# Moving small condition networks, phi matrices and a weight's transposes to other places in a planned schedule, and letting two copies choose their engine

## The chip, the cores and the metric

The kernel runs on one NeuronCore of a Trainium2 chip, as a single program in fp32. The metric is the device time of one execution in microseconds (us), lower is better. Five queues matter: TensorE (PE, matmuls and transposes into PSUM), VectorE (DVE), ScalarE (ACT, activations), GpSimd (POOL, which here also issues the indirect DMAs) and SyncE (SP, which issues the other DMAs). Each queue runs its instructions in the order in which they stand in the program; they meet through semaphores.

## The reference

Two layers, 32 samples of 256 tokens with 256 features, 8192 tokens in all. Layer 0 is a modulated linear, attention and a two-choice mixture of 8 experts with at most 2048 tokens each. Layer 1, which is where the change lies, is cut here to what it touches:

```python
# L1 attention: q and k pass through a phi matrix per head (attn_weights) and a global norm
# L1_cond2: six views of x, concatenated, then a two-layer network
def _mlp_ln(s, W1, b1, W2, b2, g, b):
    h = jax.nn.silu(s @ W1 + b1) @ W2 + b2
    return _ln(h, g, b)
m = x + _mlp_ln(memory_state, mem_W1, ...)[:, None, :]      # cond_512, 32 x 128
n = x + _mlp_ln(noise_state, noi_W1, ...)[:, None, :]       # cond_64,  32 x 64
r = x + _mlp_ln(resource_state, res_W1, ...)[:, None, :]    # fside,    32 x 32
w = jax.nn.softmax(aw)
cat = jnp.concatenate([w[0]*h, w[1]*t, w[2]*m, w[3]*n, w[4]*r, w[5]*s], axis=-1)
z = _mlp_ln(cat, int_W1, int_b1, int_W2, int_b2, int_g, int_be)
# L1 feed-forward: a linear, ten butterfly stages, gelu, ten butterfly stages, a linear
h = butterfly(z @ W_exp + b_exp, up_weights, 1024)
h = butterfly(gelu(h + up_bias), down_weights, 1024)
y = h @ W_con + b_con + down_bias
```

The three condition networks (`mem`, `noi`, `res`) work on 32 rows in all: one row per sample. Each is two small matmuls, a silu, a layer norm and a transpose.

## The kernel before, in words

**The stages.** The first stage (to about 1700 us in the trace) is layer 0's attention and routing. Then one planned section holds everything else: the expert blocks (to about 2676 us), the first pass over layer 1 (`answer`, one part per sample, to about 2847 us), a short chain that needs all samples (`norms`, global norms of q and k), and the second pass (`answer_out`, one part per sample, to the end).

**What sets the order.** All work of this section is written as Python generators, called parts. A part yields steps: an engine with an estimated length, then issues that step's instructions; a wait of an estimated length with no engine (`yield None, 2.5`); a buffer of a ring (`get`), given back with `back`; `("join", part)`, which holds the part until another part has ended. `side_by_side` plays all parts against its estimates as a list scheduler, and the order in which it lets steps go is the order of the instructions in each queue. Two engines in one yield, such as `yield (ACT, 0.7), (DVE, 0.75)`, leave the choice to it: it takes the one that ends first by its own estimates. Nothing is reordered on the chip: a step that was planned early and is ready late holds up all that stands behind it on its engine.

**Rings.** The planned section has 20 buffers `sh` of 128 x 512, 11 `big` of 128 x 2048 and 8 PSUM banks `mm`. A load of a weight into an `sh` buffer waits in SP's queue until that buffer's former user is through.

**Experts.** `expert_block` handles 512 slots: four gathers on POOL (L1529), transposes (L1539), eight hidden tiles `bh` (L1573, relu on ACT or DVE at L1560/L1562), two pairs of output tiles `by` (L1588), the bias (DVE, L1594), the gate (L1603), and four scatter-adds into the residual in memory by POOL (L1496). The scatter-adds go one at a time: each waits for the landing of the one before. All `answer` parts wait for all blocks and all scatter-adds, then load their tokens `x2` by SP (L1729) and transpose them on PE (helper `transpose2`, L246).

**What the change touches.** `butterflies` works up the two feed-forward weights during the experts; at its end it transposes the second one on PE (L1690, four groups of four) and copies it from PSUM to `w_con` on DVE (L1694). `small_tables` waits for `butterflies` and then, in one sequence: loads bias rows; computes the phi matrices `waq` and `abq` from three small weights (L1859 and L1869 on PE, copies L1864 and L1871 on DVE); loads `iw1`, the first weight of the six-view network, scales it by a softmax (ACT, L1902 to L1914; POOL, L1917, L1918); runs the three condition networks one after the other (loads L1927 to L1932; PE L1937, L1946, L1963; silu on ACT L1941; DVE L1952 to L1954, L1959, L1967; the power -1/2 on POOL, L210 and L216); and adds them up into `bvec` (PE L1979, DVE L1986). Every network holds five `sh` buffers. `norms` waits for all of `answer`, `squares`, `small_tables` and `butterflies`.

`answer_out` does, per sample: two projections (L266), softmax-like features, a layer norm, side views `t` and `s` on POOL (L2047, L2049) and `h` on DVE, transposes of `x`, `t`, `s`, `h` (L246), the copy of `h` from PSUM (DVE, L2134), 16 matmuls over the six-view weight (L2147), silu (ACT, L2156), a projection, a layer norm (`un`), its transposes, the scale and bias of `zT` from PSUM (DVE, L2175), 16 matmuls `dh` with gelu (L2198, L2188), 16 matmuls `do` (L2212) and the output. Up to four samples are in flight.

Of the kernel before, what the change touches and what calls it, by code (L numbers as in the profile page):

```python
# [14 lines left out]
F = mybir.dt.float32  # L15
# [7 lines left out]
P = 128  # L23
S = 256
D = 256
# [144 lines left out]
def network(ctx: ExitStack, tc: tile.TileContext, a: dict, out: bass.AP):  # L170
# [113 lines left out]
    def back(r):  # L284
        return "back", rings[r][2]
# [1354 lines left out]
    def butterflies(after):  # L1640

        for p in after:
            yield "join", p
        xb = yield from get("big", "bfb", [1, FF])
        yield SP, 0.1
        nc.sync.dma_start(w_eff, a["wexp"].rearrange("(c p) f -> p c f", p=P))
        yield SP, 0.1
        nc.sync.dma_start(xb, a["bexp"])
        for st in range(NST):
            w = yield from get("big", "bfw", [P, FF // 2, 2, 2])  # L1650
            yield SP, 0.1
            nc.sync.dma_start(
                w.rearrange("p k i j -> p (k i j)"), a["upw"][st : st + 1, :].to_broadcast([P, 2 * FF])
            )
            yield DMA, 5.3
            yield None, 2.0
            for x in (w_eff[:, 0, :], w_eff[:, 1, :], xb):
                yield from butterfly_stage(x, w, 1 << st, False)
            yield back("big")

        ps = yield from get("mm", "mm", [P, 8])
        yield PE, 0.6
        for f in range(8):
            nc.tensor.matmul(
                ps[:, f : f + 1], xb[0:1, f * P : (f + 1) * P], ones[0:1, 0:1], start=True, stop=True
            )
        yield DVE, 0.2
        nc.vector.tensor_add(b_eff, ps, cols[:, C_UPB : C_UPB + 8])
        yield back("mm")
        yield back("big")  # L1670
        xw = yield from get("big", "bfx", [P, 2, FF])
        yield SP, 0.1
        nc.sync.dma_start(xw, a["wconT"].rearrange("(c p) f -> p c f", p=P))
        for st in reversed(range(NST)):
            w = yield from get("big", "bfw", [P, FF // 2, 2, 2])
            yield SP, 0.1
            nc.sync.dma_start(
                w.rearrange("p k i j -> p (k i j)"), a["dnw"][st : st + 1, :].to_broadcast([P, 2 * FF])
            )
            yield DMA, 5.3  # L1680
            yield None, 2.0
            for c in range(2):
                yield from butterfly_stage(xw[:, c, :], w, 1 << st, True)
            yield back("big")
        for f in range(0, 8, 2):
            ps = yield from get("mm", "mm", TS)
            yield PE, 0.55
            for g in range(2):
                for c in range(2):
                    nc.tensor.transpose(  # L1690
                        ps[:, g, c * P : (c + 1) * P], xw[:, c, (f + g) * P : (f + g + 1) * P], ident
                    )
            yield DVE, 0.7
            nc.vector.tensor_copy(w_con[:, f : f + 2, :], ps)  # L1694
            yield back("mm")
        yield back("big")

# [128 lines left out]
        yield back("big")  # L1826
        yield back("big")

    def small_tables():

        yield "join", weights_part
        yield "join", matrices
        yield SP, 0.1
        nc.sync.dma_start(rowsD, a["rows_d"][:, :N_ROWS_D].to_broadcast([P, N_ROWS_D]))
        bb = yield from get("sh", "bb")
        yield SP, 0.1
        nc.sync.dma_start(
            bb.rearrange("p t d -> p (t d)"), a["rows_d"][:, N_ROWS_D : N_ROWS_D + 2 * D].to_broadcast([P, 2 * D])
        )
        yield None, 2.5  # L1840
        yield DVE2, 0.5
        nc.vector.tensor_add(bcon, bb[:, 0, :], bb[:, 1, :])
        yield back("sh")
        yield POOL, 0.1
        nc.gpsimd.memset(qacc, 0.0)

        blk = yield from get("sh", "blk", [P, 2, P])
        yield SP, 0.1
        nc.sync.dma_start(blk, a["ablk"].rearrange("(k p) m -> p k m", p=P))
        for n in ("aq", "ak"):  # L1850
            nat = yield from get("sh", "nat")
            yield SP, 0.1
            nc.sync.dma_start(nat, a[n].rearrange("(k p) i -> p k i", p=P))
            yield None, 2.5
            for i in range(2):
                ps = yield from get("mm", "mm", TS)
                yield PE, 0.9
# [15 lines left out]
            yield back("sh")  # L1873
        yield back("sh")


        awr = wD.tile([P, 6], F, name="awr")
        wsm = wD.tile([P, 6], F, name="wsm")
# [2 lines left out]
        awo = ROWS_S["aw"][0]  # L1881
        yield SP, 0.1
        nc.sync.dma_start(awr, a["rows_s"][:, awo : awo + 6].to_broadcast([P, 6]))
        condin = {}
        for n, src, k in (("mem", "condT", P), ("noi", "noiT", 64), ("res", "resT", 32)):
            if n == "mem":
                condin[n] = condT
            else:
                condin[n] = wD.tile([k, B], F, name="ci_" + n)
                yield SP, 0.1  # L1890
                nc.sync.dma_start(condin[n], a[src])
        iw1 = []
        for i in range(2):
            t = yield from get("big", "iw1", [P, 6, D])
# [20 lines left out]
        for k in range(2):  # L1915
            yield POOL, 1.3
            nc.gpsimd.tensor_add(wcat[:, 6 + k, :], iw1[4 + k], iw1[6 + k])  # L1917
            nc.gpsimd.tensor_add(wcat[:, 6 + k, :], wcat[:, 6 + k, :], iw1[8 + k])  # L1918
        vT = {}
        for n in ("mem", "noi", "res"):  # L1920
            ci = condin[n]
            k = ci.shape[0]
            m1 = yield from get("sh", "m1", [k, D])
            m2 = yield from get("sh", "m2")
            rb = yield from get("sh", "rb", [B, D])
            yield SP, 0.1
            nc.sync.dma_start(m1, a[n + "W1"])  # L1927
            yield SP, 0.1
            nc.sync.dma_start(m2, a[n + "W2"].rearrange("(k p) n -> p k n", p=P))
            o, w_ = ROWS_S[n + "b2"]  # L1930
            yield SP, 0.1
            nc.sync.dma_start(rb, a["rows_s"][:, o : o + w_].to_broadcast([B, w_]))  # L1932
            yield None, 2.5
            ps = yield from get("mm", "mm", TS)
            yield PE, 0.4
            for m in range(2):
                nc.tensor.matmul(ps[:, m, :B], m1[:, m * P : (m + 1) * P], ci, start=True, stop=True)  # L1937
            hT = yield from get("sh", "mhT", [P, 2, B])
            yield ACT, 1.8
            for m in range(2):  # L1940
                nc.scalar.activation(hT[:, m, :], ps[:, m, :B], AF.Silu, bias=col(n + "b1", m))  # L1941
            yield back("mm")
            ps = yield from get("mm", "mm", TS)
            yield PE, 0.9
            for c in range(2):
                nc.tensor.matmul(ps[:B, 0, :], hT[:, c, :], m2[:, c, :], start=(c == 0), stop=(c == 1))  # L1946
            u = yield from get("sh", "mu", [B, D])
            st = sm.tile([B, 6], F, name="mst")
            mv = sm.tile([B, 2], F, name="mmv")
            rstd = sm.tile([B, 1], F, name="mrs")  # L1950
            yield DVE, 1.1
            nc.vector.tensor_add(u, ps[:B, 0, :], rb)  # L1952
            nc.vector.bn_stats(st, u)
            nc.vector.bn_aggr(mv, st)  # L1954
            yield back("mm")
            yield POOL, 0.8
            rsqrt(rstd, mv[:, 1:2], 1, LN_EPS)
            yield DVE, 0.4
            nc.vector.tensor_scalar(u, u, mv[:, 0:1], rstd, ALU.subtract, ALU.mult)  # L1959
            ps = yield from get("mm", "mm", TS)  # L1960
            yield PE, 0.3
            for c in range(2):
                nc.tensor.transpose(ps[:, c, :B], u[:, c * P : (c + 1) * P], ident[:B, :B])  # L1963
            vT[n] = wD.tile([P, 2, B], F, name="vT_" + n)
            yield DVE, 0.3
            for c in range(2):
                nc.vector.tensor_scalar(  # L1967
                    vT[n][:, c, :], ps[:, c, :B], col(n + "g", c), col(n + "be", c), ALU.mult, ALU.add
                )
            yield back("mm")  # L1970
            for _ in range(5):
                yield back("sh")
        ps = yield from get("mm", "mm", TS)
        yield PE, 1.6
        for m in range(2):
# [84 lines left out]
    def answer_out(b, begin, before):  # L2060
# [69 lines left out]
        yield PE, 0.55  # L2130
        transpose2(ps, h2)
        cT["h"] = yield from get("sh", "cT_h", TS)
        yield DVE, 0.7
        nc.vector.tensor_copy(cT["h"], ps)  # L2134
        yield back("mm")
        yield back("sh")
        for p in (px, pt, ps_):
# [32 lines left out]
        transpose2(ps, un)  # L2170
        yield back("sh")
        zT = yield from get("sh", "zT", TS)
        yield DVE, 0.9
        for c in range(2):
            nc.vector.tensor_scalar(  # L2175
                zT[:, c, :], ps[:, c, :], col("intg", c), col("intbe", c), ALU.mult, ALU.add
            )
        yield back("mm")


        yield "rank", B
        gT = yield from get("big", "gT", [P, 8, S])

        def gelu(ps, f0):
# [51 lines left out]
    table_part = Part(small_tables())  # L2236
    first_parts = [Part(answer(b)) for b in range(B)]
    square_part = Part(squares() if NG > 0 else iter(()))
    norm_part = Part(norms([*first_parts, square_part, table_part, matrices]))
    with tc.manual_schedule():  # L2240
        side_by_side(
            [routed, weights_part, *loads[:2], matrices, *blocks, *loads[2:], table_part, *first_parts, square_part, norm_part]
# [126 lines left out]
```

## Time and profile before

| | us |
|---|---|
| median of 3 runs | 3804.84 (3804.16 to 3808.98) |
| the profiled execution, its own time | 3813.55 |
| its span in the profile | 3811.8 |
| PE busy in the span | 3516.6 (92%) |
| DVE / ACT / POOL busy | 2519.2 (66%) / 1796.2 (47%) / 1810.6 (48%) |

The granted TensorE clock has a mean of 0.97 over the span. Read the page as follows: part 1 gives the busy time of each engine; part 2 cuts the span into 40 slices and shows where an engine is not full; part 4 follows the chain that ended last. PE is the fullest engine and carries 41% of that chain. In part 2 its row has the digit 9 nearly everywhere after the first slices and 8 or 7 in two places: around 1700 us, where routing is, and in the slices from 2600 us and from 2800 us, on both sides of the first pass over layer 1.

A matmul or a transpose in fp32 is recorded as two matmul records, except transposes, of which there is one per instruction; the time that a group of them takes from PE is best read from the distance between the starts of neighbouring rows, since their ends are modelled.

### The profile page before, as it was taken

Reading aid. Unit: us, or ns where it says so; the run is one execution under the profiler, and the core shown is the slowest. Engines: PE = TensorE matmul, PEld = TensorE weight load, DVE = VectorE, ACT = ScalarE, POOL = GpSimd, SP = SyncE. Lnnn points to the kernel's source line nnn. Section 1 sums busy time; section 2 is a strip of 40 time slices with the busy share of each in tenths; the row PEclk is TensorE's granted clock in tenths of the full one; section 3 lists DMA queues with packets and bytes.
Section 4 is the critical chain, followed back from the end, with each engine's and each line's share of the span. In section 5 each row is a group of like instructions: output and inputs, shape, how many; then the busy total and the mean of one; then the engine's idle time right before and its main releaser. Section 6 shows DMA issues by size and latency. Waiting matters only on the chain.

```text
span 3811.8 us, 55412 instructions
## 1 busy us (share of the span) xinstructions
PE 3516.6 (92%) x22001; PEld 2582.0 (68%) x22001; DVE 2519.2 (66%) x4296; ACT 1796.2 (47%) x2714; POOL 1810.6 (48%) x1291
## 2 busy tenths in 40 slices
PE   3899999999999999987999999999898999999999
PEld 2566666666666666654666666666787888888888
DVE  7999998899898899746665551000336656565654
ACT  2677777777777777752222222222332333333333
POOL 3436543544544444415555565553125556565553
PEclk7999999999999999987999999999999999999999
DMA  1001000000100000004333333322341233222321
GB/s 63 18 29 33 30 30 22 26 31 27 30 30 30 30 30 25 25 18 156 88 85 102 82 97 76 65 43 38 117 163 56 100 96 109 91 92 91 122 92 42
DMA packets 136494, 241.43 MB, mean 63 GB/s; under 512 B 19265, under 2 KB 80897, under 8 KB 133666
## 3 DMA queue, kind: packets, MB, share of 16 engines
q0 software_dynamic: 48128, 100.77, 10.8%
q1 hardware_dynamic: 87954, 136.51, 10.7%
q8 instruction: 176, 2.88, 0.3%
q14 instruction: 92, 0.75, 0.1%
q10 hardware_dynamic: 144, 0.52, 0.0%
HBM read 187.25 MB, written 50.48 MB: 62 GB/s over the span
## 4 chain that ended last, share of the span: by engine, by line
PE 41%; DVE 5%; issue 4%; POOL 3%; DMA 1%; ACT 0%; SPq 0%; POOLq 0%; DVEq 0%; ACTq 0%
PE by L1588 11%; PE bh L1573 11%; PE do L2212 4%; PE mm L2147 4%; PE dh L2198 3%; PE mm L266 3%; PE mm L246 1%; PE mm L258 1%; PE gram L1762 1%; PE mm L1539 1%; DVE st L315 1%; POOL ga L2035 1%; DVE v L2110 1%; DVE hh L2049 0%; POOL gc L2035 0%
## 5 line engine op out<-in xcount | busy, mean ns | idle before, releaser
L975 ACT ACTIVATE pt<-sc 128x2048 f32<-128x2048 f32 x256 | 481.1, 1879 | 160.1 <-PE sc L966 157.3
L216 POOL TENSOR_TENSOR n<-n,negh 128x32 f32<-128x32 f32 x64 | 377.1, 5893 | 200.9 <-DVE n L827 151.6
L216 POOL TENSOR_TENSOR rstd<-rstd,negh 128x2 f32<-128x2 f32 x160 | 146.0, 914 | 673.3 <-DVE rstd L317 668.9
L1562 ACT ACTIVATE hid<-bh,cols 128x512 f32<-128x512 f32 x256 | 175.2, 688 | 599.2 <-PE bh L1573 586.1
L1588 PE MATMUL by<-w,hid 128*128 128x256 f32 x2048 | 454.5, 380 | 2.5 <-DVE ysb L1594 2.5
L1573 PE MATMUL bh<-ehT,w 128*128 128x512 f32 x1024 | 451.4, 594 | 1.3 <-DVE ysb L1594 1.3
L1588 PEld LDWEIGHTS by<-w,hid 128*128 128x128 f32 x2048 | 387.6, 191 | 67.2 <-issue 14.4
L948 PE MATMUL av<-pt,vaug 128*32 128x256 f32 x4096 | 280.7, 392 | 81.0 <-ACT pt L975 73.9
L1594 DVE TENSOR_TENSOR ysb<-by,b 128x512 f32<-128x512 f32 x64 | 44.0, 688 | 457.0 <-PE by L1588 379.8
L1573 PEld LDWEIGHTS bh<-ehT,w 128*128 128x128 f32 x1024 | 194.7, 191 | 221.3 <-issue 215.2
L1496 POOL DMA_INDIRECT rrows<-ysb,row x128 | 220.5, 1723 | 256.9 <-DMA rrows<-ysb,row 148.5
L786 DVE TENSOR_TENSOR hprod<-hprod 128x1024 f32<-128x1024 f32 (+2 forms) x384 | 319.4, 832 | 6.5
L966 PE MATMUL sc<-qT,kT 32*128 32x256 f32 x4096 | 299.2, 407 | 6.1 <-ACT pt L975 6.0
L778 DVE TENSOR_TENSOR hprod<-hex,kk 128x2048 f32<-128x2048 f32 x128 | 296.3, 2315 | 0.0
L966 PEld LDWEIGHTS sc<-qT,kT 32*128 32x128 f32 x4096 | 188.2, 187 | 104.0 <-issue 88.2
L948 PEld LDWEIGHTS av<-pt,vaug 128*32 128x32 f32 x4096 | 108.2, 110 | 208.7 <-ACT pt L975 118.8
L2198 PE MATMUL dh<-zT,w_eff 128*128 128x256 f32 x1024 | 237.2, 381 | 6.7 <-DVE zT L2175 6.7
L2212 PE MATMUL do<-w_con,gT 128*128 128x256 f32 x1024 | 232.6, 381 | 0.0
L1529 POOL DMA_INDIRECT xg<-h2buf,tok x128 | 152.3, 1190 | 162.9 <-issue 55.8
L2198 PEld LDWEIGHTS dh<-zT,w_eff 128*128 128x128 f32 x1024 | 190.2, 191 | 31.3 <-DVE zT L2175 7.9
L2212 PEld LDWEIGHTS do<-w_con,gT 128*128 128x128 f32 x1024 | 194.0, 192 | 25.6
L735 DVE TENSOR_REDUCE hex<-hprod 128x64 f32<-128x1024 f32 (+1 forms) x192 | 176.1, 948 | 2.4
(615 smaller groups left out, 7128.7 us busy)
## 6 DMA issues: line engine op xcount, KB each, us to landing
w<-in_w SPq DMA_DIRECT2D x16, 1024.0 KB
x<-rrows SPq DMA_DIRECT2D x64, 256.0 KB
bfw<-in_upw SPq DMA_DIRECT2D x10, 1024.0 KB
bfw<-in_dnw SPq DMA_DIRECT2D x10, 1024.0 KB
xT<-in_xT SPq DMA_DIRECT2D x32, 256.0 KB
x<-in_x SPq DMA_DIRECT2D x32, 256.0 KB
ugbb<-gtab SPq DMA_DIRECT2D x32, 256.0 KB
h2buf<-xh SPq DMA_DIRECT2D x32, 256.0 KB
```

The lines of the kernel that those rows point to most:

```text
L216: nc.gpsimd.tensor_tensor(o, o, negh[:p].to_broadcast([p, n]), ALU.pow)
L735: nc.vector.tensor_reduce(e[:, t, j0 : j0 + n, :] if exact else e[:, t, 8:, j0 : j0 + n].rearrange("p h j -> p j h"), pr[:, t].rearrange(" ...
L778: nc.vector.tensor_tensor(pr.rearrange("p j (h d) -> p j h d", d=DH), weights(t, j0, 8)[:, 0].unsqueeze(3).to_broadcast([P, 8, H, DH]), wi ...
L786: nc.vector.tensor_tensor(pr[:, :n], pr[:, :n], pr[:, n : 2 * n], ALU.add)
L948: nc.tensor.matmul(av[32 * i : 32 * i + 32, c % 2, :], va[:, kc, 4 * c + i, :], pt[:, i, kc, :], start=(kc == 0), stop=(kc == 1),)
L966: nc.tensor.matmul(sc[:, i, kc, :], kT[r, m, kc * P : (kc + 1) * P], qT[r, e, m, :], start=True, stop=nm is None,)
L975: nc.scalar.activation(pt, sc, AF.Exp, scale=1.0 / math.sqrt(DH))
L1496: nc.gpsimd.indirect_dma_start(rrows[:, :], bass.IndirectOffsetOnAxis(ap=row[:, j0 + t : j0 + t + 1], axis=0), y[:, t, :], None, compute_o ...
L1573: nc.tensor.matmul(ps, w["w1"][:, c, f * P : (f + 1) * P], hT[c], start=(c == 0), stop=(c == 1))
L1588: nc.tensor.matmul(ps[:, t, :], hid[f // 4][:, f % 4, (t0 + t) * P : (t0 + t + 1) * P], w["w2"][:, f, :], start=(f == 0), stop=(f == 7),)
L2198: nc.tensor.matmul(ps[:, g, :], w_eff[:, c, f * P : (f + 1) * P], zT[:, c, :], start=(c == 0), stop=(c == 1))
L2212: nc.tensor.matmul(ps[:, t, :], gT[:, f, t * P : (t + 1) * P], w_con[:, f, :], start=(f == 0), stop=(f == 7))
```

## The change

- The phi part of `small_tables` becomes a part of its own, `phi_weights`. Its loads are issued first, and its PE work joins the last expert block (`blocks[-1]`).
- The three condition networks become parts of their own, `condition_network`, which run beside each other. Their loads are issued early; their PE work, too, joins the last expert block. Their instructions are the same.
- `small_tables` no longer waits for `butterflies`, but for the fourth block from the end (`blocks[-4]`); it starts the networks and the phi part, then goes on with `iw1` and its scaling, and joins them before `bvec`.
- In `butterflies`, the transposes of the second linear wait for the first `NG + 2` parts `answer` (30 of 32), and their copies move from DVE to ACT. `norms` no longer waits for `butterflies`; each `answer_out` does, ahead of its gelu.
- In `answer_out` two copies out of PSUM, `cT_h` and `zT`, may go to DVE or ACT.

```diff
@@ butterflies
+        for p in first_parts[: NG + 2]:
+            yield "join", p
         for f in range(0, 8, 2):
...
-            yield DVE, 0.7
-            nc.vector.tensor_copy(w_con[:, f : f + 2, :], ps)
+            yield ACT, 0.6
+            nc.scalar.copy(w_con[:, f : f + 2, :], ps)
@@ small_tables, its phi part
-        yield "join", weights_part
-        yield "join", matrices
...
+    def phi_weights():
         blk = yield from get("sh", "blk", [P, 2, P])
...
+        yield None, 2.5
+        yield "join", blocks[-1]
+        for n, nat in zip(("aq", "ak"), nats):
@@ small_tables, its networks
+    def condition_network(n, src, k, vT):
...
+        m1 = yield from get("sh", "m1", [k, D])
+        m2 = yield from get("sh", "m2")
+        rb = yield from get("sh", "rb", [B, D])
...
+        yield None, 2.5
+        yield "join", blocks[-1]
+        ps = yield from get("mm", "mm", TS)
+        yield PE, 0.4
...
+    def small_tables():
+        yield "join", weights_part
+        yield "join", blocks[-4]
...
+        vT = {}
+        nets = [Part(condition_network(*n, vT)) for n in (("mem", "condT", P), ("noi", "noiT", 64), ("res", "resT", 32))]
+        for p in nets:
+            yield p
+        phis = Part(phi_weights())
+        yield phis
...
-        for n in ("mem", "noi", "res"):
...
+        for p in (*nets, phis):
+            yield "join", p
@@ answer_out
-        yield DVE, 0.7
-        nc.vector.tensor_copy(cT["h"], ps)
+        engine = yield (DVE, 0.7), (ACT, 0.6)
+        if engine == ACT:
+            nc.scalar.copy(cT["h"], ps)
+        else:
+            nc.vector.tensor_copy(cT["h"], ps)
...
-        yield DVE, 0.9
+        engine = yield (DVE, 0.9), (ACT, 1.0)
         for c in range(2):
...
+            if engine == ACT:
+                nc.scalar.activation(
+                    zT[:, c, :], ps[:, c, :], AF.Identity, bias=col("intbe", c), scale=col("intg", c)
+                )
...
         yield "rank", B
+        yield "join", matrices
         gT = yield from get("big", "gT", [P, 8, S])
@@ network
-    norm_part = Part(norms([*first_parts, square_part, table_part, matrices]))
+    norm_part = Part(norms([*first_parts, square_part, table_part]))
```

## Prediction, on record before the run

> **What bounds the kernel now.** I read the page first: PE is busy 92% of the span and carries 41% of the chain that ended last, so a stage gets shorter only where PE gets less to do or waits less. Then I cut the span into stretches of 100 us and looked for those where PE is not full. The columns are the stretch, its length, the busy time of PE, PEld, DVE, ACT and POOL, the granted clock, the DMA share and GB/s.
>
> ```profile
> 2500.00:2600.00 100.00, 100.00 (x362) 66.36 (x361) 9.30 (x21) 23.32 (x35) 51.18 (x43) 1.00 0.28 48
> 2600.00:2700.00 100.00, 86.41 (x345) 62.71 (x344) 12.35 (x33) 28.36 (x54) 29.19 (x25) 0.91 0.23 45
> 2700.00:2800.00 100.00, 98.56 (x599) 86.86 (x597) 37.85 (x88) 29.36 (x69) 13.89 (x43) 1.00 0.45 151
> ```
>
> The experts (2500) and the first pass over layer 1 (2700) are full. Between them lies a hole. PE's own order of time shows it (start, duration, line, work, count; in brackets the idle time before and who ended it):
>
> ```profile
> 2660.03 0.61 PE L1859 MATMUL mm<-blk,nat 128*128 128x128 f32 x4
> 2660.48 7.07 PE L1588 MATMUL by<-w,hid 128*128 128x256 f32 x32
> 2667.39 0.50 PE L1869 MATMUL mm<-cols,blk 128*128 128x1 f32 x4
> 2667.75 7.15 PE L1588 MATMUL by<-w,hid 128*128 128x256 f32 x32
> 2674.74 1.05 PE L1859 MATMUL mm<-blk,nat 128*128 128x128 f32 x8
> 2675.63 0.51 PE L1869 MATMUL mm<-cols,blk 128*128 128x1 f32 x4
> 2688.94 1.97 PE L246 MATMUL mm<-ident,x 128*128 128x128 f32 x8 [12.81 <-DMA x<-rrows]
> ...
> 2700.71 0.53 PE L1937 MATMUL mm<-condT,m 128*128 128x32 f32 x4
> 2701.07 0.63 PE L252 MATMUL mm<-ident,yT 128*128 128x128 f32 x4
> ...
> 2703.36 1.05 PE L1946 MATMUL mm<-m,mhT 128*32 128x256 f32 x4
> 2704.34 1.58 PE L1762 MATMUL gram<-y 128*128 128x257 f32 x8
> ```
>
> The last expert tile ends at 2674.74 and the first token tile of layer 1 is there at 2688.94. What sets this is not PE: the last four scatter-adds start at 2668.94, 2673.42, 2677.85 and 2682.35 on POOL, each after the landing of the one before, SP issues the loads at 2686.32, and they land 2.6 us later. So PE work put into this hole is free, and the same work in the full stages around it is not. The reader is to see that two pieces of phi (L1859, L1869) stand in full stretches before the hole, and all of the networks (L1937 and on) in the full stretch after it.
>
> The last stage, 2884 to the end, has smaller holes. PE's waits there (who waited for whom: us in total, times, longest):
>
> ```profile
> PE dh L2198 <- DVE zT L2175: 6.7, 3, 2.2
> PE mm L246 <- POOL s L2049: 5.7, 9, 1.9
> PE mm L246 <- DVE h L2049: 5.6, 4, 1.7
> PE mm L246 <- POOL t L2049: 3.3, 3, 1.8
> PE mm L246 <- DVE un L238: 3.2, 4, 1.1
> PE mm L246 <- POOL x L2112: 2.8, 5, 0.7
> ```
>
> Together 27.3 us of 928. A zT stall in its place: PE ends the transposes of `un` near 3319.1, but DVE has two `hh` steps queued first (the second takes 1.64), so zT starts at 3320.90.
>
> **Phi matrices.** From the starts of neighbouring rows: 0.45 (2660.03 to 2660.48), 0.36 (2667.39 to 2667.75) and a first group at 2632.04, 0.44. These 1.25 us leave the full stage. The rest of phi, 1.4 us after 2674.74, lies in the hole already. Gain 1.25. Its DVE copies (0.42 and 0.15 each) move into the hole, where DVE is nearly idle.
>
> **Networks.** One network costs PE 0.36 (L1937), 0.98 (L1946, 2703.36 to 2704.34) and 0.23 (L1963, 2708.61 to 2708.84) = 1.57; three cost 4.71, in a stage where PE is 98.6% busy. In the built order of the changed kernel all three stand behind the last `by`, except for one last L1963 and one L1859, which stand behind five token tiles: 0.23 + 0.36 stay. Gain 4.71 - 0.59 = 4.1.
>
> Does the chain hold up the token tiles, which stand behind it on PE? Count from the end of the last `by`, T. The built order puts the three powers on POOL behind the last scatter-add, whose issue ends at T + 9.2 (2683.90). A power is 0.18 + 0.58, two take 1.7; DVE's normalization is 0.40, PE's transposes follow. The second transposes, the last thing ahead of the tiles, are reached near T + 11.8; the tiles land at T + 14.2 or a little later. Slack about 2.5 us: cost 0. The third network follows behind five tiles and is then ready (its power near T + 13.5).
>
> Everything else that a network issues: three or four loads on SP (0.3 to 0.6 each). They now stand ahead of `iw1` and wait for `sh` buffers: in the built order the last such wait is for the pair of scatter-adds that landed at 2592.78 in this trace, the very event that let SP go on to `iw1` before. So `iw1` lands about as before (DMA falls idle again near 2604.5), plus some 1.2 us for 0.4 MB more. Silu (0.28 each, six) and its table load (1.28) leave the busy pass for the hole.
>
> **`iw1`.** Its 12 scalings (4.89) and six copies (1.92 in the rows of ACT) and four POOL adds (0.72 to 1.31) ran in the hole; the built order puts them ahead of the relus of the block before the last. ACT has 7.5 us free there (it ends at 2605.41 and needs its next relu at 2612.88), POOL 8.0 us before its next scatter-add (2612.52). What falls there, 6.0 us (two scalings come earlier) and 3.5, fits: cost 0. Without that cover, the relus would wait for ACT by up to 6 us.
>
> **Transposes of the second linear.** 16 at 0.11 us = 1.76 us (2296.56 to 2296.99 for four). They leave a full stage, but in the built order they stand ahead of the last squares of the first pass, which is full as well. Net 0 (from -1.8 if they meet a pause to +2.4 if the four ACT copies, 0.59 each by the row of `y`, delay the last squares; nearer to 0, since ACT waits 18 us for PE there).
>
> **A rule about the clock.** In this trace the granted clock drops within the hole and stays low into the pass:
>
> ```profile
> 2676.00:2678.00 2.00, 0.13 (x2) 0.05 (x1) 1.56 (x9) 0.30 (x1) 0.15 (x1) 1.00 0.28 41
> 2680.00:2682.00 2.00, 0.00 (x0) 0.00 (x0) 0.00 (x0) 2.00 (x6) 0.00 (x0) 0.50 0.54 64
> 2692.00:2694.00 2.00, 1.83 (x9) 1.46 (x8) 0.00 (x0) 1.34 (x4) 0.00 (x0) 0.50 0.82 290
> ```
>
> Eight transposes take 1.97 us there against 1.04 elsewhere, so 24 of them lose about 3 us. The Trainium skill, "TensorE: Matmul & The Clock Gate", Part 1, says that the clock halves after an idle window of about 3.4 us and returns after about 3.4 us of sustained work. If the moved work kept the clock up, the sum would gain 3 us more. But it falls into a burst to about T + 4 and short pieces near T + 11; the 6 to 7 us between exceed both the rule and the row. I take no gain, and 0.6 us loss for the small pieces that now run at half clock ahead of the first `xmT` matmuls.
>
> First part of the sum: 1.25 + 4.1 - 0.6 = 4.8 us (3 to 8).
>
> **The copies on either engine.** In the built order 12 of 32 `cT_h` and 10 of 32 `zT` go to ACT. A `cT_h` is 0.59 there (cT_t) against 0.69 on DVE; a half of `zT` 0.57 (nearest row: hT, from PSUM with scale and bias) against 0.53. DVE (about 59% busy here) loses 12 x 0.69 + 10 x 1.06 = 19 us, ACT (about 34%) takes 18 us. That alone is worth nothing; it counts where it alters a stall. And it alters the order: before, the stalls of zT (3 x 2.23) and h (1.70, 1.46, 1.70) come from a sequence that PE repeats from about 3310 on; after, PE repeats a sequence near to the one that ran from 2999 to 3150, which had none of these. That could take off 11.5 us, and 3.7 us at the passage between the two (t 1.82, s 1.92 at 3166 to 3168). Against it, the new sequence puts the transposes of `s` right behind `t` once more in each six samples; `s` is ready 2.5 us after `t` on POOL, so up to 2.1 us in each of five repeats comes back. Bounds -15 and +10 (that with no zT or h stall saved). Since a removed stall mostly lets something else be late, I take -6.
>
> ACT's table loads speak to this as well: the trace has 1.283 us for each, with the next ACTIVATE right behind it (3306.37 + 1.28, then 3307.67). "ScalarE: Activation LUTs", What ACT_TABLE_LOAD costs, puts a switch at 2.66 us with its drain. The built order has 71 in the last stage instead of 91, and none ahead of a zT. By the row that frees 26 us of ACT, by the rule 53; the row decides, and ACT isn't the bound, so 0.
>
> **Sum.** 4.8 + 6 = 10.8 us. The profiled execution, 3813.55 (span 3811.8), would become 3802.7; the median of the runs lies 8.7 lower, so 3804.84 - 10.8 = 3794.
>
> **Rivals.** *Only the hole pays* (0.29): the last stage is bound by POOL's side views and by DVE's layer norms, both unchanged, and the stalls come back under other names. For it: POOL's s, t and x are 11.8 of the 27.3 us. Gain 4.8, or 3800; within 0.2%. That the two copies do nothing is the same case. *ACT holds its queue* (0.06): in the built order five of the ten zT stand ahead of a gelu table load and of gelus that are due. If such a zT waits for late `un` transposes, the gelus wait, then `do`. At 2.2 us in each of the ten, against 4.8 won, the time is 3804.84 + 22 - 4.8 = 3822; it decides from 0.5 us each on, and exceeds 0.2% from 1.2. Against it: `do` never waits for gelu in this trace (idle before L2212 0.0). *Likeliest* (0.65): both parts pay, 3794.
>
> A measurement of this kernel can tell about 0.2%, 7.6 us, from no change. Of the likeliest case a little falls below that, of the first rival some above: faster 0.65, same 0.29, slower 0.06. The range reaches to 3784 (last stage at -16) and to 3804 (last stage at +4).
>
> **What would show it.** Right: the first tile's wait falls from 12.8 us to pieces, with L1887, L1896 and L1849 in the hole; the pass from first tile to `norms` is some 4 us shorter; no stalls of 2.2 at dh. Wrong: the first token tile starts later than 14.5 us after the last `by` (the chain or a load holds it); PE idle in the last experts (late `iw1`); or PE's waits in the last stage are still 27 us or more.

## The result and the profile after

The kernel after takes 3797.52 us (median; 3785.77 to 3799.91), measured beside the kernel before at 3804.50: a ratio of 0.9976, with a 95% interval of 0.9968 to 0.9984, or 9.1 us less (6.1 to 12.2; the two medians differ by 7.0). On a second chip the ratio was 0.9975 (0.9967 to 0.9984). The profiled execution of after took 3797.68 us (span 3795.9), which is its median; that of before, 3813.55, lay 9 us above its own median. So the 15.9 us between the two profiles overstate the change, and the stages have to be compared one by one:

| stage (by PE's order of time), us | before | after |
|---|---|---|
| experts, first L1573 to end of last `by` | 921.3 | 919.3 |
| hole, to the first token tile | 14.0 | 14.7 |
| first pass, to the matmul of `qs` | 159.2 | 152.3 |
| from there to the first matmul with `wcat` | 36.7 | 35.7 |
| last stage, to the end of the span | 926.9 | 922.4 |

These stages hold 13.7 of the 15.9 us; the other 2.2 stand ahead of the first expert tile (at 1753.6 and 1751.4 us), where the change touches nothing.

The hole is filled. The same stretches of 100 us as shown of before, here of after:

```profile
2600.00:2700.00 100.00, 93.47 (x386) 68.34 (x384) 18.79 (x51) 26.47 (x54) 32.37 (x40) 0.93 0.23 40
2700.00:2800.00 100.00, 100.00 (x608) 90.77 (x607) 36.15 (x77) 30.78 (x71) 13.56 (x31) 1.00 0.49 166
```

PE has 93.47 us of work in the stretch with the hole, 86.41 before, and is now full in the next. PE's order of time in after, from the end of the last expert tile:

```profile
2670.57 0.53 PE L1887 MATMUL mm<-condT,m 128*128 128x32 f32 x4
...
2672.78 1.05 PE L1896 MATMUL mm<-m,mhT 128*32 128x256 f32 x4
...
2676.91 0.71 PE L1849 MATMUL mm<-blk,nat 128*128 128x128 f32 x4
2681.75 0.42 PE L1913 MATMUL mm<-ident,mu 32*128 32x32 f32 x2 [4.13 <-DVE mu L1909]
...
2685.48 1.94 PE L246 MATMUL mm<-ident,x 128*128 128x128 f32 x8 [1.81 <-DMA x<-rrows]
```

The networks (L1887, L1896) and phi (L1849) run to 2677.6, then PE waits for the first normalized result of a network, `mu` (4.13 us) and, ahead of the tile, 1.81 us for the tile's load. What was one wait of 12.8 us is in pieces, and the load still ends the hole, not the chain.

PE's waits in the last stage of after (who waited for whom: us in total, times, longest):

```profile
PE mm L246 <- POOL s L2061: 13.4, 10, 1.9
PE mm L266 <- DMA dyT<-ytbuf: 10.2, 6, 2.1
PE dh L2219 <- DVE zT L2195: 1.7, 1, 1.7
PE mm L246 <- DVE un L238: 1.4, 2, 1.0
```

Of the stalls of before, `h` and the three zT of 2.2 us are gone, as are `t` and `x`. In their place `s` takes 13.4 us, and `dyT`, which nobody waited for before, takes 10.2. With 0.2 for `hsT` the sum is 26.9 us against 27.3.

### The profile page after: what moved, and what is told of

Read it like the earlier page. It is cut to its first block, busy times and chain, and to the rows that moved or that the text cites. A ratio compares the mean times of both kernels' runs of the same rounds, so it can differ in the third digit from the quotient of the medians.

```text
span 3795.9 us, 55431 instructions
## 1 busy us (share of the span) xinstructions
PE 3510.1 (92%) x22001; PEld 2578.9 (68%) x22001; DVE 2500.0 (66%) x4266; ACT 1783.1 (47%) x2724; POOL 1808.3 (48%) x1291
## 3 DMA queue, kind: packets, MB, share of 16 engines
q0 software_dynamic: 48128, 100.77, 10.9%
q1 hardware_dynamic: 87954, 136.51, 10.9%
## 5 line engine op out<-in xcount | busy, mean ns | idle before, releaser
L1573 PE MATMUL bh<-ehT,w 128*128 128x512 f32 x1024 | 452.3, 595 | 1.4 <-DVE ysb L1594 1.4
L1573 PEld LDWEIGHTS bh<-ehT,w 128*128 128x128 f32 x1024 | 195.1, 191 | 222.2 <-issue 214.8
```

What stands on the lines that cost most here:

```text
L1573: nc.tensor.matmul(ps, w["w1"][:, c, f * P : (f + 1) * P], hT[c], start=(c == 0), stop=(c == 1))
```

## The experiments

Two theories are set against each other. Theory H says that the gain is the hole (and what PE no longer does in the full stages), while the last stage only trades stalls, one for another. Theory L, which is half of my sum, says that the new order of the last stage pays about as much as the hole. Ratios are to the kernel before on the same chip.

**Only what goes into the hole** (`hole_only`). The kernel after with the copies and the transposes of the second linear undone (and `norms` joining `matrices` again):

```diff
-        for p in first_parts[: NG + 2]:
-            yield "join", p
-            yield ACT, 0.6
-            nc.scalar.copy(w_con[:, f : f + 2, :], ps)
+            yield DVE, 0.7
+            nc.vector.tensor_copy(w_con[:, f : f + 2, :], ps)
...
-        yield "join", matrices
...
-        engine = yield (DVE, 0.7), (ACT, 0.6)
+        yield DVE, 0.7
...
-        engine = yield (DVE, 0.9), (ACT, 1.0)
+        yield DVE, 0.9
```

> Only the networks, phi and iw1 are moved; the two copies stay on DVE, the transposes of the second linear stay where they were. Built, the last stage then has the very sequence of PE of the kernel before. Theory H (the gain is the hole: networks and phi out of the full stages, and the 2.2 us wait for y that stood in the first pass): 3797 to 3799, a ratio of 0.998; first pass about 150 to 152 us long against 159.2, last stage 927 as before with its stalls of zT (3 x 2.2) and h. Theory L (the new order of the last stage pays, as half of my sum had it): 3800 to 3801, and the kernel after stays 3 us or more below this one.

Measured: 3798.17 us, ratio 0.9981 (0.9974 to 0.9987), 7.2 us less (4.9 to 9.9). First pass 152.0 us, hole 14.7, and in the last stage the stalls of before:

```profile
PE dh L2208 <- DVE zT L2185: 6.7, 3, 2.2
PE mm L246 <- DVE h L2059: 5.7, 4, 1.7
```

Its own waits there come to 26.7 us. Its profiled execution, 3808.20 us, was the slowest of its 21; below, its first pass is compared without waits and half clock. By the ratios most of the gain, 7 of 9 us, is here without any change of the last stage. The 2 us that are left to the rest lie within the intervals.

**Only the transposes of the second linear** (`wcon_only`). The kernel before with the join ahead of the transposes, the copies on ACT, the join of `matrices` moved to zT, and `small_tables` joining `blocks[-4]`:

```diff
+        for p in first_parts[: NG + 2]:
+            yield "join", p
...
-            yield DVE, 0.7
-            nc.vector.tensor_copy(w_con[:, f : f + 2, :], ps)
+            yield ACT, 0.6
+            nc.scalar.copy(w_con[:, f : f + 2, :], ps)
...
-        yield "join", matrices
+        yield "join", blocks[-4]
```

> Only the transposes of the second linear are moved behind the first pass's tiles, with their copies on ACT, and the networks' joins adapted to it. Theory H: PE has 1.76 us more in the first pass and 1.76 less in the experts, so no change, 3803 to 3806, ratio 0.9995 to 1.0005. A rival, that waits for these copies had held the experts: 3801 or less.

Measured: 3804.95 us, ratio 1.0001 (0.9993 to 1.0009). No change, as the prediction had it.

**All but those transposes** (`hole_copies`). Of the diff above, all but the two `engine` hunks.

> The whole change but for the transposes of the second linear. Built, the last stage has the very sequence of the kernel after. Theory H: the same as the kernel after to 2 us (3796 to 3799), since the transposes are worth nothing; and within 2 us of hole_only, since the last stage only trades its stalls (zT and h 11.5 us against s and dyT some 12). Theory L: 3 us or more below hole_only.

Measured: 3798.19 us, ratio 0.9976 (0.9965 to 0.9986). That is the ratio of after, and its waits in the last stage have the same names: s 13.4, dyT 11.6. Against `hole_only`, on the same chip, the copies and the new order bring 2 us (0.9976 and 0.9981), within the intervals. The 3 us or more of theory L are not shown. In the profile its last stage took 931.0 us against 922.4 in after, though both have the same order there; what differs is the clock, told below.

The copies alone were not run. The plan of the kernel before with these two hunks alone gives ACT the same 12 `cT_h` and 10 `zT`, and PE's order in the last stage is then that of after. So the copies alone make the new order, and the hole has no part in it; what they are worth is read from `hole_copies` against `hole_only`.

**The new order, all copies on DVE** (`order_on_dve`):

```diff
         engine = yield (DVE, 0.7), (ACT, 0.6)
+        engine = DVE
...
         engine = yield (DVE, 0.9), (ACT, 1.0)
+        engine = DVE
```

> The kernel after with its order of work unchanged, but the 12 copies of cT_h and the 10 of zT that ACT took are issued on DVE at the same place of the order. If the order alone makes the last stage what it is: the same as the kernel after to 2 us, 3796 to 3799, no zT stall of 2.2. If ACT's share of the copies is what removes the stalls of zT: these come back, at 1 to 2.2 us for each of ten zT, 3805 to 3815.

Measured: 3802.12 us, ratio 0.9991 (0.9984 to 0.9998), some 5.7 us above `hole_copies` on the same chip (the intervals overlap a little). PE's order in the last stage is that of after. Its largest waits there:

```profile
PE mm L246 <- POOL s L2061: 13.4, 10, 1.9
PE mm L266 <- DMA dyT<-ytbuf: 11.1, 6, 2.8
PE mm L246 <- POOL x L2124: 2.9, 4, 0.7
PE dh L2221 <- DVE zT L2197: 1.7, 1, 1.7
```

No stall of zT came back, so it is the order that removed those. But a stall of `x` (2.9) that after does not have is there, and that of dyT is 0.9 longer. ACT's share of the copies is worth these 3.8 us and perhaps a little more. Neither expectation came true: the time lies between their ranges.

**Why dyT is late** (`gathers_half`). In after, POOL issues twelve table gathers in a row, two samples' sets, five times: from 2987, 3161, 3337, 3511 and 3685. Five of the six stalls of dyT follow one of these (3007.8, 3183.4, 3357.7, 3531.8, 3705.6). In the kernel before this happens once. Around one of them, in after's order of time (SPq and POOL issue, PE waits):

```profile
3173.69 0.39 SPq L2243 DMA_DIRECT2D out<-xo  x1
3174.24 0.79 SPq L2082 DMA_DIRECT2D dyT<-ytbuf  x1
3175.20 0.95 POOL L2047 DMA_INDIRECT ga<-in_msgb,ids  x1 [0.30 <-issue]
3183.40 1.97 PE L266 MATMUL mm<-wav,dyT 128*128 128x256 f32 x8 [1.84 <-DMA dyT<-ytbuf]
```

The load of dyT is issued at 3174.24, behind the store of `xo`, while the last of the twelve gathers is issued at 3175.20; PE can go on 9.2 us after the load's issue. The median from issue to landing is 3.1 us for the loads of dyT in this stage. From 3173 to 3178 the DMA engines are busy 0.99 of the time, from 3183 on 0.01. The experiment leaves the order as it is and takes bytes away:

```diff
+                if n != "ct" and b >= 4:
+                    nc.gpsimd.memset(gt[n][:, t, :], 0.5)
+                    continue
                 nc.gpsimd.indirect_dma_start(
```

> The kernel after with the gathers of two of the three tables (pw and ms, half of the gathered bytes) left out from the fifth sample on, POOL filling their place with a constant, so that what the side views compute is not the reference. The order is unchanged, also SP's. If dyT is late because its load shares the DMA engines with two samples' gathers in a row: its stalls in the last stage fall from 10.2 us to 4 or less, those of s change by what POOL's fills take less or more time. If it is late because SP issues it late, behind the store of xo: the stalls of dyT stay at 10 us.

Measured: 3771.07 us, ratio 0.9892 (0.9877 to 0.9907). All of PE's waits in its last stage:

```profile
PE mm L246 <- POOL s L2064: 4.1, 5, 0.8
PE dh L2222 <- DVE zT L2198: 1.7, 1, 1.7
PE mm L246 <- DVE un L238: 1.5, 2, 1.1
```

The stalls of dyT are gone, with SP's order as it was: at the same place of the sequence SP issues the load 7.2 us before PE needs it, and 7.3 us in after. So it was the gathers that made it late, not SP. Whether it is their bytes, their number or the time at which POOL issues them, this run does not separate. The fill takes POOL about 0.5 us where a gather took 0.95 and 0.30 of issue, and with POOL earlier the stalls of `s` fall to 4.1 too.

**Costs of the plan** (`plan_costs`). The planner reckons 1.1 us for a gather and 1.3 for each step of `t` and `s`. POOL's rows in after:

```profile
3328.96 1.77 POOL L2059 TENSOR_TENSOR t<-dxh,gc 128x512 f32<-128x512 f32 x1 [0.85 <-DVE dxh L238]
3330.81 1.60 POOL L2061 TENSOR_TENSOR t<-t,gc 128x512 f32<-128x512 f32 x1
3332.37 1.26 POOL L2059 TENSOR_TENSOR s<-dxh,ga 128x512 f32<-128x512 f32 x1
```

The steps of `t` take 1.65 and 1.55 in the mean, those of `s` 1.27 at the same shape; so `s` is ready later than planned, and PE, whose order is fixed, waits for it.

```diff
-                yield POOL, 1.1
+                yield POOL, 1.25
...
-        x = yield from modulated(POOL, name, xh, gt, n, i, 1.3)
+        x = yield from modulated(POOL, name, xh, gt, n, i, 1.65 if name == "t" else 1.3)
```

> The kernel after, with two costs of the plan set to what the trace shows: a table gather on POOL 1.25 us (0.95 and 0.30 between them) for 1.1, and each of the two steps of t 1.65 (rows: 1.65 and 1.55) for 1.3. No instruction is changed, only their order: built, PE's sequence becomes a repeat of two samples without two gathers' sets in a row and without the transposes of s right behind those of t. Theory H (the last stage of the kernel after only trades stalls, and s and dyT are what it paid with): the stalls of s (13.4 us) and of dyT (10.2) fall below 8 together, the time to 3778 to 3786. A rival, that stalls come back under other names whatever the order is: PE's waits of the last stage stay at 24 us or more, 3795 to 3800.

Measured: 3783.95 us beside a kernel before of 3812.28 on this chip; ratio 0.9928 (0.9915 to 0.9942), 27 us less. The kernel before is slower on this chip than on the first (3804.50), so this overstates it. The kernel after with doubled networks, told below, took 3799.42 here, and after itself 3797.52 on the first chip; against these two the plan's costs bring 14 to 16 us on top of the change. Largest waits of its last stage:

```profile
PE mm L246 <- DVE un L238: 10.9, 14, 1.6
PE mm L266 <- ACT hsT L2171: 1.0, 2, 0.6
PE mm L246 <- POOL s L2061: 0.8, 1, 0.8
...
PE mm L266 <- DMA dyT<-ytbuf: 0.5, 1, 0.5
```

s and dyT fell from 23.6 us to 1.3. A part came back as `un` (1.4 to 10.9), so the sum of waits is 14.4 and not 3. The gathers now come in sixes, but for one twelve at 2987. With these costs the planner gives ACT only 5 of the `cT_h` and 2 of the `zT`.

**The plan's costs without the change** (`plan_before`, `plan_hole_only`, with `after_again` on their chip). The same two lines in the kernel before and in `hole_only`.

> The kernel after once more, on the same chip as the next three, since the kernel before differs by up to 8 us from chip to chip. Both theories: a ratio of 0.9965 to 0.9985 to the kernel before.

> The kernel before with the two plan costs set to what the trace shows (gather 1.25, steps of t 1.65), nothing else. If what the last stage can win lies in the plan's costs and not in the change: 12 us or more below the kernel before, ratio 0.997 or less, though its built order is not the clean repeat of two samples. If only the change's copies on either engine open the way to it: within 5 us of the kernel before.

> The two plan costs together with the moved networks and phi, the two copies on DVE and the transposes of the second linear where they were. Its last stage has the order of the run before it here (plan costs alone). If hole and plan costs add up: 7 us below that run. If the copies on either engine are worth something once the plan's costs are right: the kernel after with the plan costs (0.9928) stays 5 us or more below this one.

Measured: `after_again` 3795.99 us, ratio 0.9975; `plan_before` 3793.57, 0.9968 (0.9956 to 0.9980); `plan_hole_only` 3786.35, 0.9948 (0.9935 to 0.9962). So the plan's costs alone are worth 12.2 us (7.6 to 16.7), no less than the change (9.5, 6.1 to 12.6); the hole adds 7.6 us to that, about the same as without them (the intervals overlap a little). What the copies add is not shown: 0.9928 against 0.9948 would be 7.6 us, but 0.9928 is of the chip where the kernel before is slower; on the chip of these three `plan_costs_fill` below stands at 0.9935, 4.9 us less, with overlapping intervals. In the profiles the waits of the last stage are 19.3, 16.7 and 14.4 us with these costs.

**Twice the networks** (`nets_twice_before`, `nets_twice_after`). Each matmul of the networks is done twice:

```diff
-        for m in range(2):
+        for m in (0, 1, 0, 1):
             nc.tensor.matmul(ps[:, m, :B], m1[:, m * P : (m + 1) * P], ci, start=True, stop=True)
...
-        for c in range(2):
+        for c in (0, 1, 0, 1):
             nc.tensor.matmul(ps[:B, 0, :], hT[:, c, :], m2[:, c, :], start=(c == 0), stop=(c == 1))
```

> The kernel before, where each matmul of the three networks (L1937 and L1946 there) is done twice with the same result; the order is unchanged. That is 3 x (0.36 + 0.98) = 4.0 us more of PE in the full first pass. Theory H: 4 us longer, 3808 to 3809, ratio 1.001. A rival, that the pass has slack for it (waits for transfers that this fills): 3804 to 3806.

> The same doubling in the kernel after, where the networks stand in the hole. Theory H: the added 4.0 us fall into PE's 9 us of idle time there, only what lies on the chain to the second L1913 counts (about 3.3 us ahead of it, against a slack of about 2 us ahead of the token tiles): first tile at 14.7 to 16.5 us after the last by, time 0 to 1.5 us above the kernel after, 3797 to 3799. If the hole isn't free: 4 us above it, 3801 to 3802.

Measured: in before 1.0012 (1.0004 to 1.0021), 4.6 us more, where 4.0 was worked out. In after 3799.42 us at 0.9962 (0.9948 to 0.9975), not above the 0.9976 of after, which is of another chip. The firmer sign is in the trace: its first tile stands 14.6 us after the last `by`, as in after (14.7). The same work costs its full length in the pass and delays nothing in the hole. In this execution the clock was also up for the tiles. One stretch of after, then two of this kernel:

```profile
2692.00:2694.00 2.00, 2.00 (x5) 1.64 (x6) 0.46 (x2) 0.42 (x2) 0.00 (x0) 0.50 0.00 0
2676.00:2678.00 2.00, 2.00 (x6) 0.71 (x4) 0.00 (x0) 0.00 (x0) 0.39 (x1) 0.50 0.54 62
2692.00:2694.00 2.00, 2.00 (x11) 1.75 (x10) 1.05 (x3) 0.00 (x0) 0.00 (x0) 1.00 0.00 0
```

The granted clock (third column from the end) is halved within the hole, where no tile is late for it, and full at 2692, where after shows 0.50.

**Both together** (`plan_costs_fill`): `plan_costs` with the doubled matmuls.

> The kernel after with the plan costs, and the networks' matmuls done twice as in the doubling above, which kept the granted clock up in the hole. If the 3 us of half clock on the first token tiles are to be had: first pass 150 to 151 us against 154, time 1 to 4 us below the kernel after with the plan costs, ratio 0.9918 to 0.9925. If the half clock only moves: the same ratio, 0.9928, or above.

Measured: 3781.66 us beside 3805.92; ratio 0.9935 (0.9922 to 0.9949). Not below 0.9928; the clock was at half again from 3 to 10 us after the first tile. So the doubling does not hold the clock in each execution, and whether it is worth anything stays open. `plan_costs`, this one and `plan_hole_only` are the versions that beat both kernels.

## Why the prediction was right, and which step of it failed

**The time.** 3794.0 was forecast, with 3784 to 3804; 3797.5 came. Faster by over 0.2% held narrowly (0.24%). That the sum came out is luck in part: the hole paid about 2.4 us more than its 4.8, the new last stage about 4 us less than its 6, and these two errors nearly cancel.

**Phi and networks, 4.8 us.** Right in its mechanism, and low: `hole_only` gained 7.2 (4.9 to 9.9). The doubled matmuls show the price of 4.0 us in the pass and none in the hole. If the waits and the half clock are taken off each profile's first pass, 150.1 us of before (159.2 - 4.0 - 5.1) become 144.2 in `hole_only` (152.0 - 2.3 - 5.5), 5.9 less, where 4.1 was worked out; `plan_before` against `plan_hole_only` and `hole_copies` gives 149.6 and 144.4 to 144.5. Of this, 4.6 us are the moved rows themselves. I took the first matmuls of one network, 0.36, for all three; those of the other two take 0.56:

```profile
2713.39 0.63 PE L1937 MATMUL mm<-ci_noi,m 64*128 64x32 f32 x4
2713.95 1.99 PE L258 MATMUL mm<-xmT,cw 128*128 128x256 f32 x8
```

The other 0.7 to 1.3 us stay open. After comes to 145.9 (152.3 - 1.5 - 4.9), with the transposes of the second linear, 1.76, in it: 4.2 less than before. The rest of the 6.9 us by which after's pass is shorter lies in before's profile: it has a wait of 2.2 us for `y`. I had not priced that, and it isn't the change's: such a wait, of 1.6 to 4.0 us, stands in 4 of the 14 traces, in kernels of both kinds. What causes it stays open. The experts became 2.0 us shorter, where 1.25 and 1.76 left them.

**The chain ahead of the tiles.** Right. I put the second L1913 at T + 11.8 and the tile at T + 14.2; they stand at 12.5 and 14.7 after the end of the last `by`. PE still waits 1.81 us for the load, so the slack is 1.8 and not 2.5.

**The half clock of the tiles.** I took 0.6 us. In before the clock was back 6.7 us after the first tile, in after 9.9, and half of that time is lost: 3.37 against 4.93 us, 1.6 more. In `hole_copies` it was back after some 4. So it is a loss here, and no larger than what differs between executions of one order.

**iw1 and the transposes of the second linear, 0.** Right: PE's idle time in the experts is 4.0 us where it was 3.8, and `wcon_only` is at 1.0001.

**The copies "alone worth nothing".** Wrong by a little: in the new order ACT's share of them removes 3.8 us of waits (`order_on_dve`).

**The last stage, 6 us. This step failed.** I said that the stalls of zT, h and the passage, 11.5 and 3.7 us, would vanish, and that `s` right behind `t` would cost up to 2.1 us in each of five repeats. The first is as measured. The second was mis-sized: there are two such stalls in a repeat, 1.91 and 0.81, and `s` went from 5.7 to 13.4 us. And a third was not seen: I judged the new sequence by the stretch of before from 2999 to 3150. Twelve gathers in a row come there too, once, from 2998.0, but the load of dyT is issued 10.4 us behind the first of them (3008.4) and is in time. In after this comes every six samples, the load is issued 11.6 to 13.3 us behind the first gather and is late, and dyT takes 10.2 us. Waits fell by 0.4 us, not by 6. "Since a removed stall mostly lets something else be late" was the right reason, and the rival *Only the hole pays* describes the last stage as it came; the hole paying more than 4.8 put the time between that rival's 3800 and my 3794.

**The rivals.** *ACT holds its queue* is refuted: dh waited for zT once, 1.7 us, and `do` for gelu never. *Only the hole pays* blamed POOL's side views as a bound that nothing moves. That part fell as well: with two true costs in the plan they are nearly gone.

**Why profiles of one order differ by 9 us.** In the last stage a sum holds: its length is about 894 us, plus PE's waits, plus 1.7 us for each stretch of half clock. The seven traces that are not in the table leave 893.9 to 896.7 us.

| last stage, us | length | PE's waits | half-clock stretches x 1.7 | rest |
|---|---|---|---|---|
| before | 926.9 | 27.3 | 5.1 | 894.5 |
| `hole_only` | 929.7 | 26.7 | 8.5 | 894.5 |
| after | 922.4 | 26.9 | 1.7 | 893.8 |
| `after_again` | 924.8 | 26.0 | 5.1 | 893.7 |
| `hole_copies` | 931.0 | 28.5 | 8.5 | 894.0 |
| `plan_costs` | 909.3 | 14.4 | 0 | 894.9 |
| `gathers_half` | 900.7 | 7.3 | 0 | 893.4 |

So the 4.5 us between the last stages of the two profiles are 0.4 of waits, 3.4 of clock and 0.7 of neither.

## What to carry to other kernels

Work moved from a stage where an engine is full into a pause that a transfer sets is worth its length, and can be priced ahead from the rows; count only the chain that must end ahead of the transfer. A new order of a nearly full stage is not worth the stalls that it removes: for each of its repeats, list which transfers and which slower engine's results now stand close together, and price these as well. Where an order is planned from costs, compare the costs with the trace first: two of them, off by 0.15 and 0.3 us, were worth as much here as the whole change.

## What was not expected of the hardware

**Short waits halve the clock, if they fall right.** In the last stages of all 14 traces there are 25 places where the granted clock fell to 0.50, mostly for 3.4 us, or 1.7 us lost. From the hole on, all changes of the clock in a trace lie on one grid of 3.41 us. Cut the last stages into the stretches of this grid, 3635 in all: PE's rows leave 1.90 us or more idle in 27 of them, and the clock fell right behind 25 of these. It fell behind no other; the idlest of those has 1.84 us. So a wait of 1.9 to 2 us is enough when it lies within one stretch, and does nothing when the grid cuts it in two. Of 30 waits of 1.5 to 1.8 us none halved the clock, of 35 from 1.8 to 2.2 twelve did, of 20 longer ones thirteen. In `plan_costs` no wait exceeds 1.6 us, and there is no such place. The Trainium skill, "TensorE: Matmul & The Clock Gate", Part 1, names an idle window of about 3.4 us for it, and says that the window runs freely. The length of a stretch and the free running agree; the idle time that suffices is shorter here, 1.9 of 3.41 us. As the grid lies elsewhere in each execution, what a wait of 2 us costs is a matter of chance. That fits what one kernel's runs differ by: after took 3785.77 us at a mean clock of 0.974, 3799.91 at 0.970.

**Loads behind gathers.** In after a load of dyT (256 KB) lands 3.1 us after its issue in the median, and 9.2 and 9.3 us after it (at 3522.5 and 3348.2) when it is issued behind nine of twelve gathers.

**POOL and DVE beside each other.** While POOL works on `t`, DVE works on `hh`: its second step took 1.64 us there against 0.69 for the first, and the steps of `t` 1.77 and 1.60 against 1.26 for `s`, all on 128x512. In four of before's 30 samples POOL has no step of `t`, `s` or `x` beside it, and there the second step takes 0.69 as well. That they slow each other fits; no run took one of them away.
